# Layer 1's short form moved into layer 0's branch, with PE's order pinned and fillers in its waits

## The chip, the cores and the metric

The kernel runs on one core of a Trainium2 chip. The metric is the device time of one execution in microseconds (us). The engines are TensorE (PE in the profile; its weight loads are PEld), VectorE (DVE), ScalarE (ACT), GpSimd (POOL) and SyncE (SP), which issues most of the DMAs.

## The reference, cut to what matters

Four layers work on 2048 tokens of 256 features; each adds to the tokens what a conditioning step and a feed-forward step make of them.

```
x = x + L0_ffn(L0_cond(x, cond))     # 32 experts, top 1, and a shared expert
x = x + L1_ffn(L1_cond(x, cond, mask))
x = x + L2_ffn(L2_cond(x, cond))     # shared and routed experts, twice
x = x + L3_ffn(L3_cond(x, cond))     # shared and routed experts, then 16 experts
```

Layer 1 matters here. Its conditioning is an attention whose query is the same for all tokens of a batch of 1024:

```
a    = einsum('bhe,bhse->bhs', tp, q)          # tp: the condition
qmod = broadcast(einsum('bhs,bhse->bhe', a, q))  # one query for all
attn = softmax(where(mask, qmod.k / sqrt(e), neg))
o    = einsum('bhts,bhse->bhte', attn, v) @ Wo.T
```

Where all rows of the mask are equal, every token of a batch gets the same row `o`. Layer 1's feed-forward (a gate over 16 experts with q, k, v and o projections, and a causal attention with weights that sum to one) then also gives one row for each of the two batches. Layer 1 so comes down to two rows, each added to 1024 tokens. The kernel computes at run time whether the rows of the mask differ.

## The kernel before, in words

The tokens lie in SBUF twice: XT by channel (two halves of 128 channels, 2048 tokens) and Xt by token (16 tiles of 128 tokens by 256). A "ring" of 20 pieces of SBUF takes the weights of all layers in turn. The kernel is written in a tile framework: it tracks the data between instructions and puts in the semaphore waits. Each engine runs its own instructions in order. A scheduler sets that order, within one block between branches, from priorities that follow the order of the program; `_behind` pins one instruction after another with an order-only dependency. A branch ends the block on all engines: each jumps by itself, and the scheduler moves nothing across it.

Layer 0 (`_layer0`, from L385) computes the experts' logits and gives every expert 96 rows; `_route_static` also returns `nov`, how many of 21 overflow slots the tokens beyond 96 per expert need. Blocks 0 and 1 of the shared expert run (`shared(tb)`, 512 tokens each), then `_layer1_pre` (L593), which prepares what layer 1 needs of its weights and computes `differ`, the count of places in which the mask's rows differ. Then come 24 static slots (L470 to L483; `Split` does the matmuls, L1475 to L1493). Behind them `n` is loaded into a register on every engine (L484) and nested branches follow (`more`, L486 to L494): three overflow slots in each, as far as `n` goes. With these inputs `n` is 0: the slots' tokens are gathered into `xs` 138 times in all, 24 for layer 0's slots and 114 for the later layers'. Every engine jumps over the overflow code once.

Then layer 1's expert weights are loaded (`_layer1_experts`, L579: 16 loads of 512 KB, on SP), and blocks 2 and 3 of the shared expert run, with `Combine` (L1268) in their hooks: it gathers the slots' products from `ybuf` by row, adds them to Xt on DVE and transposes Xt back to XT (`_back`, L1258: ps_bk on PE, a copy on ACT). The loop of `_shared` (L1227) is, for every 128 hidden features: spg and spu (two matmuls each, L1240), Silu on ACT to ssg (L1245), the product sa on DVE (L1247), four spo matmuls (L1250).

Then `differ` is loaded and the second branch follows (L2095 to L2109): a general layer 1, or else the short form `_layer1_one` (L674). With these inputs the short form runs. It is a chain of small steps, each a few matmuls, then DVE or ACT on the product, then the next. In order, with the tiles' names: s_pa and s_v_t, s_v_o (attention weights over tokens, `by_block` and `over_tokens`), s_v_h, s_pq, s_pw (the query), s_psc, s_pm (scores, maximum), s_z_t, s_pr1, s_z_o (softmax, weighted tokens), s_z_h, s_po, s_ph (the row `o`), s_pn, s_pl (gate: norm, logits; a chain of some thirty small DVE steps follows, L821 to L858, and ends in s_hs), s_pk (L863, 32 matmuls with the experts' projections), s_pa2, s_pqk, s_pr (L890), s_pc, s_pb. Float32 matmuls have two records each in the profile. s_pc gives the two rows by channel, s_pb by token. L903 to L909 add them: eight ACT activations with a bias on XT, two DVE additions on Xt with s_pb read from PSUM. The weights for layer 2's shared expert are loaded in the same branch (`_shared_loads`; the profile has them under `_wload`'s line, L84).

Behind the branch layer 2 begins: `_shared` on XT (spg waits for the XT activations), and on DVE some twenty small memsets and preparations of later steps (L195 to L1756).

`_consts` also makes two bf16 constants, `iota16` and `one16`, that only layer 3's last step (`Last`, L1699) reads. `_warm` (L1216) issues bf16 matmuls of an identity with itself, 512 columns, of which nothing is read; before, layer 3 alone uses it (16 of them).

Of the kernel before, what the change touches and what calls it, by code (L numbers as in the profile page):

```python
# [86 lines left out]
def _consts(k):  # L87
# [24 lines left out]
    k.iota16 = cp.tile([P, CAP], BF16, name="iota16")  # L112
    nc.vector.tensor_copy(k.iota16, ii)
# [8 lines left out]
    k.one16 = cp.tile([P, P], BF16, name="one16")  # L122
    nc.vector.memset(k.one16, 1.0)
# [261 lines left out]
def _layer0(k):  # L385
# [5 lines left out]
    xbuf, ybuf = k.xbuf, k.ybuf  # L391
    with ExitStack() as ctx:
# [49 lines left out]
        rows, eid, nov = _route_static(k, rp, psum, ixf, E, C, NOV, "l0")  # L442
# [9 lines left out]
        def shared(tb, hook=None):  # L452
            po = _shared(k, pool, psum, HT, tb, *shw, hook)
            for i in range(2):
                t = tb * 4 + i * 2
                nc.vector.tensor_tensor(Xt[:, t:t + 2, :], po[i], Xt[:, t:t + 2, :], ALU.add)

        def weights(src):
            ws = [k.ring.take().rearrange("p (c f) -> p c f", f=f) for f in (F, F, D)]
            for w, n in zip(ws, ("L0_r1", "L0_r3", "L0_r2")):  # L460
                nc.sync.dma_start(w, A[n][src].rearrange("o (c p) f -> p (o c) f", p=P))
            return ws

        for tb in range(2):
            shared(tb)
        _layer1_pre(k, k.pre, psum)
        _router_biases(k, psum)
# [15 lines left out]
        split.finish()  # L483
        n = nc.values_load(nov[0:1, 0:1], min_val=0, max_val=NOV)  # L484
# [10 lines left out]
        k.l1w = _layer1_experts(k)  # L495
        k.yrows = (NS + NOV) * T
# [3 lines left out]
        k.ring.drop(hold)  # L500
        c.finish()


def _route_static(k, pool, psum, ixf, E, C, nov, name):
# [46 lines left out]
    rows = pool.tile([P, NT], U32, name=name + "_rows", tag="s_rows")  # L551
# [7 lines left out]
    eid = pool.tile([1, nov], I32, name=name + "_eid", tag="s_eid")  # L559
    nc.vector.tensor_copy(eid, ef)  # L560
    n = pool.tile([1, 1], I32, name=name + "_nov", tag="s_nov")
    nc.vector.tensor_copy(n, end[0:1, E - 1:E])
    return rows, eid, n
# [15 lines left out]
def _layer1_experts(k):  # L579

    r = k.ring.take(12).rearrange("p (n i e c f) -> n i p e c f", n=3, i=4, c=2, f=P)
    for i in range(4):
        for j, n in enumerate("qkv"):
            k.nc.sync.dma_start(r[j, i], k.A["L1_p" + n][i * 4:(i + 1) * 4]
                                .rearrange("e (c p) f -> p e c f", p=P))
    o = []
    for i in range(4):
        o.append(k.ring.take().rearrange("p (e f) -> p e f", f=D))
        k.nc.sync.dma_start(o[i], k.A["L1_po"][i * 4:(i + 1) * 4].rearrange("e p f -> p e f"))
    return r.rearrange("n i p e c f -> p n i e c f"), o  # L590


def _layer1_pre(k, pp, psum):  # L593
# [6 lines left out]
    with ExitStack() as ctx:  # L600
# [19 lines left out]
        nc.tensor.matmul(pd, k.ones, d1, start=True, stop=True)  # L620
        k.differ = pp.tile([P, 1], I32, name="l1_differ")
        nc.vector.tensor_copy(k.differ, pd)
# [51 lines left out]
def _layer1_one(k):  # L674
# [5 lines left out]
    l1w, l1o = k.l1w  # L680
    with ExitStack() as ctx:
        pool = ctx.enter_context(tc_pool(k, "l1s", 1))
        psum = ctx.enter_context(tc_pool(k, "l1sps", 2, PSUM))
# [27 lines left out]
        def by_block(w, name):  # L711

            ps = psum.tile([P, TB], F32, name=name, tag="b")
            for c in range(2):
                for g in range(4):
                    nc.tensor.matmul(ps[quad[g], :], w[:, c, g // 2, :], XT[:, c, g * TB:(g + 1) * TB],
                                     start=c == 0, stop=c == 1, skip_group_check=True)
            return ps

        def over_tokens(a, name):  # L720

            pt = psum.tile([P, 4, P], F32, name=name + "_t", tag="b")
            for j in range(4):
                nc.tensor.transpose(pt[:, j, :], a[:, j * P:(j + 1) * P], k.ident)
# [3 lines left out]
            ps = psum.tile([P, D], F32, name=name + "_o", tag="b")  # L728
            for j in range(4):
                for g in range(4):  # L730
                    nc.tensor.matmul(ps[quad[g], :], at[:, j, quad[g]], Xt[:, 4 * g + j, :],
                                     start=j == 0, stop=j == 3, skip_group_check=True)
            return ps

        def halves(x, name):

            ps = psum.tile([P, 2, 2, 16], F32, name=name + "_h", tag="s")
            for c in range(2):
                nc.tensor.matmul(ps[:, c].rearrange("p b h -> p (b h)"), x[:, c * P:(c + 1) * P],
                                 s2.rearrange("p b h -> p (b h)"), start=True, stop=True)  # L740
# [4 lines left out]

        pa = by_block(k.u, "s_pa")
        at = pool.tile([P, TB], F32, name="s_a")
        nc.scalar.copy(at[:, 0:256], pa[:, 0:256])
        nc.vector.tensor_copy(at[:, 256:TB], pa[:, 256:TB])
        pv = over_tokens(at, "s_v")  # L750
        vp = pool.tile([P, D], F32, name="s_vp")
        nc.vector.tensor_copy(vp, pv)
        v = halves(vp, "s_v")
        pq = psum.tile([P, 2, 2, 8], F32, name="s_pq", tag="s")
        for d in range(2):
            for c in range(2):
                nc.tensor.matmul(pq[:, d], w["q"][:, c, d * P:(d + 1) * P],
                                 v[:, c, :, 8 * d:8 * d + 8], start=c == 0, stop=c == 1)
# [3 lines left out]
        pw = psum.tile([P, 2, 2, 2, 8], F32, name="s_pw", tag="s")  # L762
        for c in range(2):
            for d in range(2):
                nc.tensor.matmul(pw[:, c, d].rearrange("p b j -> p (b j)"),
                                 k.natk[:, d, c * P:(c + 1) * P],
                                 qmd[:, d].rearrange("p b j -> p (b j)"), start=True, stop=True)
# [3 lines left out]
        psc = by_block(wk, "s_psc")  # L771
        sm = pool.tile([P, TB], F32, name="s_sm")
        mx = pool.tile([P, 1], F32, name="s_mx")
        nc.vector.tensor_tensor_reduce(sm, mb, psc, 1.0, -BIG, ALU.add, ALU.max, mx)
        pm = psum.tile([P, 1], F32, name="s_pm", tag="s")
        nc.tensor.matmul(pm, sw, mx, start=True, stop=True)
# [4 lines left out]
        pz = over_tokens(sm, "s_z")  # L781
        pr1 = psum.tile([P, 1], F32, name="s_pr1", tag="s")
        nc.tensor.matmul(pr1, sw, rs, start=True, stop=True)
# [6 lines left out]
        pov = psum.tile([P, 2, 2, 8], F32, name="s_po", tag="s")  # L790
        for d in range(2):
            for c in range(2):
                nc.tensor.matmul(pov[:, d], w["v"][:, c, d * P:(d + 1) * P],
                                 zT[:, c, :, 8 * d:8 * d + 8], start=c == 0, stop=c == 1)
# [5 lines left out]
        ph = psum.tile([P, 2, 2], F32, name="s_ph", tag="s")  # L800
        for i in range(2):
            for d in range(2):
                nc.tensor.matmul(ph[:, i, :], w["o"][:, d, i * P:(i + 1) * P], o[:, d, :],
                                 start=d == 0, stop=d == 1)
# [8 lines left out]
        pn = psum.tile([P, 2], F32, name="s_pn", tag="s")  # L813
        for c in range(2):
            nc.tensor.matmul(pn, k.ones, hq[:, c, :], start=c == 0, stop=c == 1)
        pl = psum.tile([P, 2, E], F32, name="s_pl", tag="s")
        for b in range(2):
            for c in range(2):
                nc.tensor.matmul(pl[:, b, :], hb[:, c, b, :], k.sim[:, c, :], start=c == 0, stop=c == 1)
# [39 lines left out]
        pk = psum.tile([P, 3, P], F32, name="s_pk", tag="b")  # L859
        for i in range(4):  # L860
            for c in range(2):
                for g in range(4):
                    nc.tensor.matmul(pk[quad[g]], hs[:, c, 4 * i + g, :], l1w[:, :, i, g, c, :],  # L863
                                     start=i == 0 and c == 0, stop=i == 3 and c == 1,
                                     skip_group_check=True)
# [3 lines left out]
        pa2 = psum.tile([P, 2], F32, name="s_pa2", tag="s")  # L869
        nc.tensor.matmul(pa2, pks[:, 2, :], r32[:, 0:2], start=True, stop=True)  # L870
# [3 lines left out]
        pqk = psum.tile([P, 2, P], F32, name="s_pqk", tag="s")  # L874
        nc.tensor.matmul(pqk, a4.rearrange("p g r -> p (g r)"), pks[:, 0:2], start=True, stop=True)
# [11 lines left out]
        pr = psum.tile([P, D], F32, name="s_pr", tag="b")  # L887
        for i in range(4):
            for g in range(4):
                nc.tensor.matmul(pr[quad[g], :], as_[:, 4 * i + g, :], l1o[i][:, g, :],  # L890
                                 start=i == 0, stop=i == 3, skip_group_check=True)
# [3 lines left out]
        pc = psum.tile([P, 2, 2], F32, name="s_pc", tag="s")  # L895
        for c in range(2):
            nc.tensor.matmul(pc[:, c, :], row[:, c * P:(c + 1) * P], r32[:, 0:2], start=True, stop=True)
        col = pool.tile([P, 2, 2], F32, name="s_col")
        nc.vector.tensor_copy(col, pc)
        pb = psum.tile([P, 2, D], F32, name="s_pb", tag="s")  # L900
        for b in range(2):
            nc.tensor.matmul(pb[:, b, :], ab[:, b, :], row, start=True, stop=True)
        for g in range(4):  # L903
            for c in range(2):
                x = XT[:, c, g * TB:(g + 1) * TB]
                nc.scalar.activation(x, x, AF.Identity, bias=col[:, c, g // 2:g // 2 + 1])  # L906
        for b in range(2):
            x = Xt[:, b * 8:(b + 1) * 8, :]
            nc.vector.tensor_tensor(x, x, _bc(pb[:, b, :], 1, [P, 8, D]), ALU.add)  # L909
# [306 lines left out]
def _warm(k, psum, ref, n):  # L1216

    ps = psum.tile([P, TB], F32, name="warm", tag="mm")
# [39 lines left out]
def _back(k, psum, src, dst, t, ref=None):  # L1258
# [6 lines left out]
    k.nc.scalar.copy(dst[:, :, t * P:(t + 1) * P], ps)  # L1265


class Combine:  # L1268
# [30 lines left out]
    def finish(self):  # L1299
# [894 lines left out]
```

## Time and profile before

| what | us |
|---|---|
| median of 3 runs (lowest, highest) | 1596.07 (1593.62, 1598.03) |
| the profiled execution | 1608.57 |
| its span, first to last instruction | 1606.7 |
| last layer 0 slot's matmuls (fpo, L1493) | 273.72 to 275.65 |
| first spg of shared(2) | 278.45 |
| last ps_bk of Combine | ends 329.71 |
| short form on PE, s_pa to s_pb | 334.77 to 385.94 |
| first spg of layer 2, first spo | 390.67, 397.29 |
| layer 1's loads issued by SP | 278.32 to 300.7 |

The mean granted TensorE clock of the profiled execution is 0.965 of full speed. The profiled execution is one execution, 12.5 us above the median of the runs without a profile. A group's line gives the busy time of all its instructions, the mean of one in ns, and behind the second bar the idle time of the engine ahead of them with what ended it. "issue" means that the profile shows no wait that ended it. PEldq, DVEq and so on are the sequencers of the engines, whose branch instructions are not counted as busy.

### The profile page before, as it was taken

What the parts mean: (1) busy time and instruction counts of PE and PEld (TensorE: products, weight loads), DVE (VectorE), ACT (ScalarE), POOL (GpSimd) and SP (SyncE); (2) the same over time, 40 slices, a digit from 0 to 9 for tenths busy, and PEclk for the clock granted to TensorE, in tenths of its full rate; (3) what the DMA queues carried; (4) which work ended last, traced back from release to release, by engine and by line L of the source; (5) the groups of instructions that cost most, each with busy time, mean ns of one, the idle gap of its engine ahead of it and who ended that gap; (6) DMA issues with size and microseconds to landing.
All of it is one profiled execution on the core that took longest, in us unless ns stands there. A gap on an engine that the chain in (4) does not pass through costs nothing. (4 is left out here: it accounts for less than half of the span.)

```text
span 1606.7 us, 23696 instructions
## 1 busy us (share of the span) xinstructions
PE 1484.9 (92%) x8602; PEld 1028.1 (64%) x8602; DVE 474.1 (30%) x1591; ACT 303.8 (19%) x641; POOL 285.0 (18%) x317
## 2 busy tenths in 40 slices
PE   5989998977999989999999999999999989998897
PEld 2543333533555876555599999999985548865575
DVE  3732221223411344341111111111114414446432
ACT  2312211112111212111111111111112212125222
POOL 0400000300231332023100000000000253410341
PEclk9889999977999999999999999999999999998899
DMA  9769994713211465051152354154507437662470
GB/s 251 255 206 338 345 315 157 254 54 119 81 52 40 142 214 180 27 190 53 34 179 87 119 183 150 51 181 177 177 14 266 140 121 246 193 203 92 138 242 22
DMA packets 184243, 252.47 MB, mean 157 GB/s; under 512 B 17112, under 2 KB 137824, under 8 KB 184113
## 3 DMA queue, kind: packets, MB, share of 16 engines
q1 hardware_dynamic: 164448, 210.92, 40.1%
q0 software_dynamic: 14176, 36.63, 6.3%
q10 hardware_dynamic: 5488, 3.25, 0.6%
q8 instruction: 74, 1.21, 0.3%
q14 instruction: 57, 0.46, 0.1%
HBM read 284.86 MB, written 50.76 MB: 209 GB/s over the span
## 5 line engine op out<-in xcount | busy, mean ns | idle before, releaser
L1250 PE MATMUL spo<-ring,sa 128*128 128x256 f32 x768 | 193.7, 395 | 20.2 <-DVE sa L1247 16.5
L285 POOL DMA_INDIRECT tbuf<-ys,sdst x114 | 112.3, 985 | 537.9 <-ACT ys L1453 228.4
L1250 PEld LDWEIGHTS spo<-ring,sa 128*128 128x128 f32 x768 | 141.2, 192 | 102.4 <-DVE sa L1247 75.2
L1247 DVE TENSOR_TENSOR sa<-ssg,spu 128x512 f32<-128x512 f32 x96 | 65.9, 686 | 340.8 <-PE spu L1240 289.3
L1444 PE MATMUL fpg<-xsT,ring 128*128 128x128 f32 x1152 | 141.6, 276 | 5.9 <-ACT ys L1453 5.9
L1444 PEld LDWEIGHTS fpg<-xsT,ring 128*128 128x128 f32 x1152 | 135.8, 192 | 10.4 <-ACT ys L1453 9.4
L1444 PE MATMUL fpu<-xsT,ring 128*128 128x128 f32 x1152 | 140.4, 275 | 0.0
L1444 PEld LDWEIGHTS fpu<-xsT,ring 128*128 128x128 f32 x1152 | 134.4, 192 | 0.0
L1448 DVE TENSOR_TENSOR fa<-fsg,fpu 128x512 f32<-128x512 f32 x72 | 49.5, 688 | 276.9 <-PE fpu L1444 276.9
L1451 PE MATMUL fpo<-ring,fa 128*128 128x256 f32 x576 | 130.3, 379 | 0.0
L1245 ACT ACTIVATE ssg<-spg 128x512 f32<-128x512 f32 x96 | 57.3, 597 | 348.4 <-PE spg L1240 242.8
L1451 PEld LDWEIGHTS fpo<-ring,fa 128*128 128x128 f32 x576 | 106.7, 190 | 13.0
L1240 PE MATMUL spg<-HT,ring 128*128 128x512 f32 x192 | 100.0, 608 | 5.1 <-PEq L488 2.8
L1240 PE MATMUL spg<-XT,ring 128*128 128x512 f32 x192 | 99.7, 609 | 4.7 <-ACT XT L906 4.7
L1427 PE MATMUL cpo<-ring,ch 128*128 128x256 f32 x312 | 86.7, 401 | 5.7 <-ACT ch L1424 4.1
L1240 PE MATMUL spu<-HT,ring 128*128 128x512 f32 x192 | 90.6, 592 | 0.0
L1240 PE MATMUL spu<-XT,ring 128*128 128x512 f32 x192 | 90.4, 593 | 0.0
L1421 PEld LDWEIGHTS cph<-xsT,ring 128*128 128x128 f32 x624 | 81.7, 191 | 5.0 <-ACT ch L1424 1.1
L1421 PE MATMUL cph<-xsT,ring 128*128 128x128 f32 x624 | 82.4, 275 | 0.7 <-ACT ch L1424 0.7
L1394 DVE COPY xsT<-ps_cm 128x256 f32<-128x256 f32 x138 | 56.7, 421 | 86.0 <-PE ps_cm L362 79.8
L1447 ACT ACTIVATE fsg<-fpg 128x512 f32<-128x512 f32 x72 | 43.0, 597 | 179.6 <-PE fpg L1444 179.6
L1427 PEld LDWEIGHTS cpo<-ring,ch 128*128 128x128 f32 x312 | 53.1, 189 | 20.4 <-ACT ch L1424 13.5
(570 smaller groups left out, 1601.0 us busy)
## 6 DMA issues: line engine op xcount, KB each, us to landing
ring<-in_L_w SPq DMA_DIRECT2D x108, 1024.0 KB
ring<-in_L_r SPq DMA_DIRECT2D x96, 512.0 KB
ring<-in_L_r SPq DMA_DIRECT2D x156, 256.0 KB
xs<-xbuf SPq DMA_DIRECT2D x138, 129.0 KB
ring<-in_L_W SPq DMA_DIRECT2D x32, 512.0 KB
yt<-tbuf SPq DMA_DIRECT2D x48, 256.0 KB
xbuf<-ACC SPq DMA_DIRECT2D x1, 6063.0 KB
ring<-in_L_s SPq DMA_DIRECT2D x6, 512.0 KB
```

The lines of the kernel that those rows point to most:

```text
L285: i = k.nc.gpsimd.indirect_dma_start(out=self.ap, out_offset=bass.IndirectOffsetOnAxis(ap=idx, axis=0), in_=rows, in_offset=None, **end)
L1240: mm = nc.tensor.matmul(ps, W[:, c, f * P:(f + 1) * P], X[:, c, cols], start=c == 0, stop=c == 1)
L1245: nc.scalar.activation(sg, pg, AF.Silu)
L1247: mul = nc.vector.tensor_mul(a, sg, pu)
L1250: mm = nc.tensor.matmul(po[g // 2][:, g % 2, :], a[:, g * P:(g + 1) * P], W2[:, f, :], start=f == 0 and g % 2 == 0, stop=f == nf - 1, skip ...
L1394: turned = nc.vector.tensor_copy(xT, _channel_major(k, self.psum, xs))
L1421: nc.tensor.matmul(ph[:, f, :], R1[:, c, f * P:(f + 1) * P], xT[:, c, :], start=c == 0, stop=c == 1)
L1427: nc.tensor.matmul(po, h[:, f, :], R2[:, f, :], start=f == 0, stop=f == 1)
L1444: nc.tensor.matmul(ps[:, j, :], W[:, c, (f0 + j) * P:(f0 + j + 1) * P], xT[:, c, :], start=c == 0, stop=c == 1)
L1447: nc.scalar.activation(sg, pg, AF.Silu)
L1448: nc.vector.tensor_mul(a[:, f0:f0 + 4, :], sg, pu)
L1451: nc.tensor.matmul(po, a[:, f, :], W2[:, f, :], start=f == 0, stop=f == 4 * nh - 1)
```

## The change

1. The first branch asks one combined question, `rare`: overflow slots or a mask with unequal rows. It is computed from `differ` and the total of the overflow (`end`) by two small DVE operations ahead of the slots. The Then side holds all that is seldom needed: the overflow slots, blocks 2 and 3, and a second branch for layer 1's form. The Else side holds the loads of layer 1's weights, blocks 2 and 3 with `Combine`, layer 2's loads and the short form, in one block. The order of pieces in the ring is kept; the loads alone stand inside.
2. In the short form every matmul is pinned behind the one before it (`pe`), from the last transpose of `Combine` on, and `fill(n)` puts n matmuls of `_warm` into the order: 4, 2, 1, 2, 1, 1, 1, 3, 4, 1, 2, 1, 2, 1, 14, 2, 2 and 6, 50 in all. On PE they follow: nothing (4), s_pa (2), s_v_t (1), s_v_o (2), s_v_h, s_pq, s_pw (1 each), s_psc (3), s_pm (4), s_z_t with s_pr1 (1), s_z_o (2), s_z_h (1), s_po (2), s_ph (1), s_pl (14), s_pk (2), s_pr (2), s_pb (6).
3. The two rows are copied to SBUF, into HT, which is free by then: the one by channel by DVE from s_pc, the one by token by ACT from s_pb. The additions (`_layer1_add`) stand behind the branch, common to both sides: eight ACT activations, two DVE additions from SBUF. On the general side the rows are zero.
4. `iota16` and `one16` are made in `Last`, which puts them on DVE right behind the branch, ahead of the additions on Xt.

Behind the branch the instructions are otherwise the same on every engine.

```diff
@@ _layer0
+        rare = k.pre.tile([1, 1], F32, name="l0_raref")
+        nc.vector.tensor_tensor(rare, k.differf[0:1, :], end[0:1, E - 1:E], ALU.add)
+        any_ = k.pre.tile([1, 1], I32, name="l0_rare")
+        nc.vector.tensor_copy(any_, rare)
...
+    def rest():
+        _layer1_loads(k)
         c = Combine(k, pool, psum, rows, Xt, XT, [0, 0] + [4] * 8, 2, 4)
         for tb in range(2, NB):
             shared(tb, c.hook(tb))
-        k.ring.drop(hold)
-        c.finish()
+        return c.finish()
+
+    def one(ref):
+        _shared_loads(k, k.l2, "L2_s1", "L2_s3")
+        _layer1_one(k, psum, ref)
+        _shared_loads(k, k.l2[2:], "L2_s2")
+
+    rare = nc.values_load(any_[0:1, 0:1], min_val=0, max_val=1 << 21)
+    with k.tc.If(rare > 0) as cmp:
+        with tc_pool(k, "l0p", 2) as pool, tc_pool(k, "l0ps", 4, PSUM) as psum:
+            slots_over()
+            rest()
+        differ = nc.values_load(k.differ[0:1, 0:1], min_val=0, max_val=1 << 20)
+        with k.tc.If(differ > 0) as cmp1:
+            _layer1_general(k)
+            _shared_loads(k, k.l2, "L2_s1", "L2_s3", "L2_s2")
+        with cmp1.Else():
+            with tc_pool(k, "l1sps", 4, PSUM) as psum:
+                one(None)
+    with cmp.Else():
+        with tc_pool(k, "l0p", 2) as pool, tc_pool(k, "l0ps", 4, PSUM) as psum:
+            one(rest())
+    _layer1_add(k)
@@ new
+def _layer1_sums(k):
+    return (k.HT[:, 1, 0:4].rearrange("p (c b) -> p c b", b=2),
+            k.HT[:, 0, 0:2 * D].rearrange("p (b d) -> p b d", d=D))
+
+def _layer1_add(k):
+    nc, (col, row) = k.nc, _layer1_sums(k)
+    for g in range(4):
+        for c in range(2):
+            x = k.XT[:, c, g * TB:(g + 1) * TB]
+            nc.scalar.activation(x, x, AF.Identity, bias=col[:, c, g // 2:g // 2 + 1])
+    for b in range(2):
+        x = k.Xt[:, b * 8:(b + 1) * 8, :]
+        nc.vector.tensor_tensor(x, x, _bc(row[:, b, :], 1, [P, 8, D]), ALU.add)
@@ _layer1_one
+    def pe(i):
+        nonlocal last
+        if last is not None:
+            _behind(k, i, last)
+        last = i
+
+    def fill(n):
+        nonlocal last
+        if last is not None:
+            last = _warm(k, psum, last, n, tag="o", bufs=2)
...
+        fill(4)
         pa = by_block(k.u, "s_pa")
+        fill(2)
...
         pm = psum.tile([P, 1], F32, name="s_pm", tag="t", bufs=2)
-        nc.tensor.matmul(pm, sw, mx, start=True, stop=True)
+        pe(nc.tensor.matmul(pm, sw, mx, start=True, stop=True))
+        fill(4)
...
+        fill(14)
         hn = pool.tile([P, 2], F32, name="s_hn")
...
         for b in range(2):
-            nc.tensor.matmul(pb[:, b, :], ab[:, b, :], row, start=True, stop=True)
-        for g in range(4):
-            for c in range(2):
-                x = XT[:, c, g * TB:(g + 1) * TB]
-                nc.scalar.activation(x, x, AF.Identity, bias=col[:, c, g // 2:g // 2 + 1])
-        for b in range(2):
-            x = Xt[:, b * 8:(b + 1) * 8, :]
-            nc.vector.tensor_tensor(x, x, _bc(pb[:, b, :], 1, [P, 8, D]), ALU.add)
+            pe(nc.tensor.matmul(pb[:, b, :], ab[:, b, :], row, start=True, stop=True))
+        fill(6)
+        nc.scalar.copy(rows, pb)
@@ _consts, Last.__init__
-    k.iota16 = cp.tile([P, CAP], BF16, name="iota16")
-    nc.vector.tensor_copy(k.iota16, ii)
-    k.one16 = cp.tile([P, P], BF16, name="one16")
-    nc.vector.memset(k.one16, 1.0)
+        k.iota16 = rp.tile([P, CAP], BF16, name="iota16")
+        k.nc.vector.tensor_copy(k.iota16, k.iota)
+        k.one16 = rp.tile([P, P], BF16, name="one16")
+        k.nc.vector.memset(k.one16, 1.0)
```

## The prediction

> **What bounds the kernel now.** I read the page first, for the engine that bounds; then the windows of the branches and of layer 1's short form; then its groups of instructions; last the timeline of its end.
>
> ```profile
> PE 1484.9 (92%) x8602; PEld 1028.1 (64%) x8602; DVE 474.1 (30%) x1591; ACT 303.8 (19%) x641; POOL 285.0 (18%) x317
> PEclk9889999977999999999999999999999999998899
> ```
>
> TensorE is busy for 92% of the span. The second line is the granted clock by fortieths (40.2 us each): it dips in the 9th and 10th, 321 to 402 us, where the short form lies.
>
> The windows (columns: stretch, length, busy time by engine with counts, granted clock, DMA share, GB/s):
>
> ```profile
> 278.45:300.00 21.55, 21.55 (x57) 11.13 (x58) 3.46 (x7) 2.39 (x4) 6.88 (x8) 0.92 1.03 316
> 329.72:334.77 5.05, 0.00 (x1) 0.00 (x1) 0.11 (x2) 0.40 (x2) 0.00 (x0) 0.84 0.53 208
> 334.77:338.40 3.63, 3.63 (x16) 0.59 (x16) 2.77 (x10) 0.00 (x0) 0.00 (x0) 0.50 0.04 9
> 344.00:346.60 2.60, 1.70 (x12) 1.49 (x12) 0.72 (x3) 0.00 (x0) 0.00 (x0) 1.00 0.00 0
> 346.60:356.80 10.20, 7.43 (x32) 4.11 (x32) 1.59 (x9) 1.18 (x3) 0.00 (x0) 0.51 0.00 0
> 363.80:372.45 8.65, 4.56 (x20) 4.39 (x20) 4.83 (x35) 1.72 (x3) 0.00 (x0) 0.50 0.01 2
> ```
>
> Three things are to be seen: 5.05 us before the short form in which nothing computes; a clock of about 0.50 over most of it; and a busy PE that gains nothing from being busy, since each product waits for a vector step and the next vector step for the product.
>
> The groups (busy us, mean ns | idle before):
>
> ```profile
> L863 PE MATMUL s_pk<-ring,s_hs 128*32 128x384 f32 x64 | 7.9, 662 | 3.6 <-DVE s_hs L858 3.6
> L716 PE MATMUL s_psc<-XT,s_wk 128*32 128x512 f32 x16 | 3.6, 1061 | 0.3 <-DVE s_wk L769 0.3
> L731 PE MATMUL s_z_o<-Xt,s_z_at 128*32 128x256 f32 x32 | 3.6, 634 | 0.3 <-ACT s_z_at L726 0.3
> L716 PE MATMUL s_pa<-XT,l_u 128*32 128x512 f32 x16 | 3.6, 1058 | 5.1 <-issue 5.1
> ```
>
> The branch instructions of PE's sequencer, first for layer 0's overflow (L488), then for layer 1 (L2097), durations in ns:
>
> ```profile
> L488 PEldq COMPARE_BRANCH  x1: 3348/3348/3348, 274.8 to 274.8; - x1
> ```
> ```profile
> L2097 PEldq COMPARE_BRANCH  x1: 4972/4972/4972, 329.7 to 329.7; - x1
> ```
>
> The end, from the timeline:
>
> ```profile
> 385.20 5.01 ACT L906 ACTIVATE XT<-XT,s_col 128x512 f32<-128x512 f32 x8 [2.25 <-DVE s_col L899]
> 385.97 4.49 DVE L909 TENSOR_TENSOR Xt<-Xt,s_pb 128x2048 f32<-128x2048 f32 x2 [0.81 <-PE s_pb L902]
> 390.67 3.75 PE L1240 MATMUL spg<-XT,ring 128*128 128x512 f32 x4 [4.74 <-ACT XT L906]
> 394.58 1.28 ACT L1245 ACT_TABLE_LOAD   x1 [4.37 <-PE spg L1240]
> 396.50 0.69 DVE L1247 TENSOR_TENSOR sa<-ssg,spu 128x512 f32<-128x512 f32 x1 [4.77 <-ACT ssg L1245]
> 397.29 0.89 PE L1250 MATMUL spo<-ring,sa 128*128 128x256 f32 x3
> ```
>
> PE idles 4.74 us for eight additions on ACT, then runs at half clock, and ACT loads its table only after the first spg.
>
> [...]rises at 343.2, 360.3 and 377.3 lie whole multiples of 3.41 us apart, and 344.0 to 346.6 (1.70 us of small products) was followed by 0.51.[...]
>
> **The change, part by part.** Times are on the axis of the profiled execution (span 1606.7, 1.9 us around it: 1608.57). It lies 12.5 us above the median of 1596.07; I take the difference over to the median, since no term scales with the span.
>
> *1. One branch where the first was.* [...]I price the jump at the 4.97 us row: PE goes on at 274.8 + 5.0 = 279.8 in place of 278.45, **+1.35**. Bounds: at 3.35 us, less L488's own steps, −0.3. Above, layer 1's loads: SP takes the same branch early and can issue about five 512 KB loads by 276[...]: 7 us, +3.5. DVE passed the old branch at once and now jumps too; it has some 3.1 us of layer 1's preparation (2.77 by 338.4) moved ahead: about 283. ACT's branch at 277.0 plus 6 is 283. The first spu is ready near 285, so both are hidden under PE's first products; each us beyond 285 shows in full. POOL and SP go through long before. The L2 loads stay behind the same waits on spg and spo. The two small DVE operations for the combined flag (about 0.1 us each, s_col's COPY is 0.16) lie ahead of the slots, under PE.
>
> *2. The second branch goes.* From the end of ps_bk (329.71) to s_pa were 5.06 us. Now four fillers (4 × 0.213 = 0.85; a 512-column bf16 product of L1220 takes 0.425 us each in the run of ten at half clock, 4.43 us in all, and half that at full) run while ACT copies the last XT (0.42): 0.9. **−4.15.**
>
> *3. Fifty fillers hold the clock.* Full-clock prices: 1.92 us for sixteen 32-row products of 512 columns (ps_lt, L1195), the same for 32 of 256 columns (fpo, L1493), four transposes 0.66, pk 0.082 for a record after 377.3, 0.60 for four small products, 1.05 for eight. Gains: s_pa and s_psc 1.72 each, z_o 1.71, v_o 1.32, pk 2.63, pw 0.81, ph 0.76, pn and pl 0.71, z_t 0.45, v_t 0.25, pm 0.21: 12.3 if the clock holds throughout. The fillers fit the waits at full speed: one or two (0.21, 0.43) into waits of 0.27 to 0.66, three (0.64) into 0.82, four into 1.29, fourteen (2.98) into 3.6. But between z_h and pl, about 5.6 us, there are only small products and 0.85 us of filler. The small products of 344 to 346.6 did not hold the clock, so I expect a drop there. It gives back 0.76 and 0.71, and runs the fourteen partly at half speed: entirely at half they take 5.95, 2.35 over their wait; the clock should rise on the way, so about 0.75. Together 2.2 back: **−10.1**. The like stretch v_h to pw has more filler; I let it hold (2.0 if not). Bounds −12.3 and −6.
>
> *4. The row is added behind the branch.* s_pb, at 385.94 on the old axis, is copied by ACT (0.6, as ssg) before the eight activations: 386.7 to 391.7. Then the table load 1.28 and ssg 0.6: 393.6. DVE's additions wait for that copy, 386.8 to 391.3; with 1.3 us of memsets and 0.2 us for the two moved constants it is free before 393.6. So sa at 393.6 and spo at 394.55 in place of 397.29: **−2.75**. PE needs only two of the activations and does the six spg and spu products at full clock by about 391; what is late next is ACT. The jump to the common code lies under this. Bounds −3.3 (copy and join cheap) and −1 (PE cools in its new idle time of 3 us, 1.7 us).
>
> Sum: 1.35 − 4.15 − 10.1 − 2.75 = **−15.65**: 1580.4.
>
> **Rivals.** *Full clock everywhere*: −12.3 in place of −10.1, 1578.2; with a cheap branch 1576.5. For it: at 104.1 to 107.5 PE was busy for 3.01 of 3.4 us, with small products, and kept its clock. *The clock held in the large products only[...]*: −6 for step 3, +3.5 for step 1 and −1 for step 4 are −7.65, 1588.4. *The other side: the fillers never lift the clock and become work.* At 0.425 us they exceed the waits they sit in by 5.3 us (fourteen by 2.35, four by 0.41, three by 0.45, the rest 0.1 to 0.4 each), the first four cost 0.85 more, and the products that before ran at full clock (pk's second half 2.6, pr 1.7, pqk and pa2 0.5) lose 4.8: +11, with the others' −5.55 a time of 1601.5. It decides from a clock term above +5.55. Against it: with no filler at all the dense pk raised the clock at 377.3. *The change doesn't do its work* because the fillers run outside the waits: step 3 zero, −5.55, 1590.5.
>
> **How the numbers follow.** Forecast (1577 to 1585) 0.55; full clock 0.15; weak hold[...] (1585 to 1591) 0.20; around no change, a part of the last two rivals, 0.06; the other side 0.04. A measurement can tell about 0.3% (4.8 us) from no change: faster 0.90, same 0.06, slower 0.04. The range for 8 in 10 runs from 1576 (full clock, cheap branch) to 1589[...].
>
> **What would show it.** One long COMPARE_BRANCH on PE near 275, of 3.3 to 7 us, and none near 330; s_pa within 1 us of ps_bk; s_pa, s_psc and z_o at 1.9 us rather than 3.6; a clock of 0.9 or more to z_h and a dip between z_h and pk; pk in 5.2 us; spo released by sa, with ACT's table load directly behind the last XT activation. Wrong would be: 3.6 us for these products, the fourteen fillers ending over 1 us after s_hs, sa late in shared(2), or PE idle for over 4 us before spo.

## The result, and the profile after

The changed kernel took 1587.72 us (median of 12 runs, 1582.27 to 1591.17), the kernel before beside it 1594.44 (12 runs, 1591.68 to 1599.47): a ratio of 0.9951, 95% interval 0.9934 to 0.9967, or 7.8 us less (5.3 to 10.5; the two medians lie 6.7 apart). 1580.4 had been forecast, 15.65 us less.

The page of the changed kernel and its windows (stretch, length, busy time by engine, granted clock, DMA share, GB/s):

```profile
PE 1487.3 (94%) x8652; PEld 1027.9 (65%) x8652; DVE 474.6 (30%) x1594; ACT 304.2 (19%) x642; POOL 284.4 (18%) x317
...
PEclk9889999999999999999999999999999999999899
```
```profile
273.46:278.72 5.26, 0.01 (x2) 0.03 (x1) 0.49 (x4) 0.37 (x1) 0.00 (x0) 0.85 1.17 323
329.73:330.53 0.80, 0.80 (x6) 0.20 (x3) 0.00 (x0) 0.41 (x2) 0.00 (x0) 1.00 0.73 241
...
334.30:338.70 4.40, 4.24 (x47) 2.50 (x48) 1.07 (x3) 1.28 (x1) 0.00 (x0) 1.00 0.01 4
338.70:346.00 7.30, 6.63 (x44) 2.94 (x43) 1.71 (x9) 1.13 (x3) 0.00 (x0) 1.00 0.00 0
...
350.60:360.30 9.70, 9.48 (x39) 5.41 (x38) 5.35 (x38) 1.72 (x3) 0.00 (x0) 0.65 0.01 2
...
377.30:383.00 5.70, 3.42 (x8) 2.82 (x9) 1.16 (x13) 1.45 (x2) 0.00 (x0) 0.70 0.04 15
```

The dip in the clock's line is gone. PE's gap at the branch is 5.26 us where it was 2.80, with the DMA queues full (1.17). The gap ahead of the short form is 0.80 us and filled. The clock is 1.00 through the short form but for 350.6 to 360.3, where the small products stand; it is 0.70 in the stretch around the first spo behind it.

The same products as before, in the changed kernel's groups, and its branch on PE's sequencer:

```profile
L961 PE MATMUL s_pk<-ring,s_hs 128*32 128x384 f32 x64 | 5.4, 488 | 0.0
...
L817 PE MATMUL s_z_o<-Xt,s_z_at 128*32 128x256 f32 x32 | 1.9, 382 | 0.2 <-ACT s_z_at L812 0.2
...
L799 PE MATMUL s_pa<-XT,l_u 128*32 128x512 f32 x16 | 1.9, 598 | 0.0
L799 PE MATMUL s_psc<-XT,s_wk 128*32 128x512 f32 x16 | 1.9, 598 | 0.1
```
```profile
L522 PEldq COMPARE_BRANCH  x1: 5802/5802/5802, 272.8 to 272.8; - x1
```

The end, from the timeline:

```profile
371.85 5.01 ACT L738 ACTIVATE XT<-XT,HT 128x512 f32<-128x512 f32 x8
...
372.43 4.47 DVE L741 TENSOR_TENSOR Xt<-Xt,HT 128x2048 f32<-128x2048 f32 x2
...
372.73 1.95 PE L1335 MATMUL spg<-XT,ring 128*128 128x512 f32 x4
...
376.87 1.28 ACT L1340 ACT_TABLE_LOAD   x1
...
378.80 0.69 DVE L1342 TENSOR_TENSOR sa<-ssg,spu 128x512 f32<-128x512 f32 x1 [1.02 <-ACT ssg L1340]
...
379.58 3.62 PE L1345 MATMUL spo<-ring,sa 128*128 128x256 f32 x8 [2.33 <-issue]
```

spg starts after two of ACT's eight additions, at full clock. Then sa waits for ssg, ssg for the table load, that for the eighth activation on ACT. PE idles for 2.33 us and its clock drops (0.50 from 379.52 to 382.93): the first spo takes 3.62 us, where the kernel before has 1.97.

From the end of the slots to the first spo the trace has 121.64 us before and 106.12 after: 15.5 less, against a sum of 15.65; the 1.65 us that the first spo then takes longer lie behind this stretch. The step that did not carry was from there to the kernel's time. The experiments ask where the gain comes from and why the whole kernel shows only half of it.

### The profile page after: what moved, and what is told of

It reads as the page before. It is cut to its first block, busy times and chain, and to the rows that moved or that the text cites. A ratio compares the mean times of both kernels' runs of the same rounds, so it can differ in the third digit from the quotient of the medians.

```text
span 1586.0 us, 23805 instructions
## 1 busy us (share of the span) xinstructions
PE 1487.3 (94%) x8652; PEld 1027.9 (65%) x8652; DVE 474.6 (30%) x1594; ACT 304.2 (19%) x642; POOL 284.4 (18%) x317
## 5 line engine op out<-in xcount | busy, mean ns | idle before, releaser
L1542 PEld LDWEIGHTS fpg<-xsT,ring 128*128 128x128 f32 x1152 | 135.8, 192 | 10.4 <-ACT ys L1551 9.4
```

Source lines behind the costliest of these rows:

```text
L1542: nc.tensor.matmul(ps[:, j, :], W[:, c, (f0 + j) * P:(f0 + j + 1) * P], xT[:, c, :], start=c == 0, stop=c == 1)
```

## The experiments

Theory A: the profiled execution of before had bad luck with the clock, and a usual one loses less in the short form. Rivals: the gain is made and given back behind layer 1 (B); the fillers gain little. The chips differ: the kernel before took 1592.52 us on the chip of the first four runs, 1608.17 on that of the next four, 1603.9 on that of the last, so each run is compared with the kernel before on its own chip. The expectations of the first four give times on the scale of the first pair (1594.4 and 1587.7).

**The kernel before again**, unchanged.

> The kernel before, unchanged, profiled anew. Theory A (the profiled execution of before was an unlucky one: [...]its short form ran at half clock nearly throughout, and a usual execution loses less there): about 1594.5, the stretch from s_pa to s_pb 44 to 48 us in place of 51.2, and a mean clock above 0.965. Theory B (the short form always takes 51 us in before, and what the change gains there is given back behind it): 1594.5 too, but s_pa to s_pb 50.5 to 52 us at the same clock of about 0.5, and the 12 us that this profile is above the median lie in other stages.

1593.72 us (14 runs); the profiled execution 1599.38, at 1597.5 of span. s_pa to s_pb took 51.10 us, and in two more traces of this code 51.19 and 51.18. So in every trace of before the short form is as slow as in the first. But none of these four is of a quick execution: the first lies above all twelve runs beside it, this one is the slowest of its 14, the other two the middle and the slowest of theirs. For these theory A falls; for quick executions it is untested.

**No fillers.**

```diff
     def fill(n):
-        nonlocal last
-        if last is not None:
-            last = _warm(k, psum, last, n, tag="o", bufs=2)
+        return
```

> The changed kernel without its 50 fillers, all else kept. The predicted worth of the fillers is 10.1 us: 1597.8 from 1587.7, slower than the kernel before. Theory A (half of that is luck that a usual execution has without fillers): 4 to 7 us, 1591.7 to 1594.7. Theory B (the fillers gain 10 in layer 1 and lose part behind it): 1591 to 1594 as well, but with s_pa to s_pb 50 us or more in the profile, and the stages behind spo shorter than with fillers.

1582.12 us, ratio 0.9939 (0.9916 to 0.9962): not told apart from the changed kernel's 0.9951, and below what either theory gave. Its groups on PE:

```profile
L960 PE MATMUL s_pk<-ring,s_hs 128*32 128x384 f32 x64 | 6.7, 583 | 3.6 <-DVE s_hs L955 3.6
L798 PE MATMUL s_psc<-XT,s_wk 128*32 128x512 f32 x16 | 3.6, 1061 | 0.3 <-DVE s_wk L860 0.3
L798 PE MATMUL s_pa<-XT,l_u 128*32 128x512 f32 x16 | 2.4, 598 | 0.0
L816 PE MATMUL s_v_o<-Xt,s_v_at 128*32 128x256 f32 x32 | 1.9, 382 | 0.5 <-ACT s_v_at L811 0.5
```

Without any filler, and with no jump ahead of them, s_pa and s_v_o run at full clock: 1.00 from 326.61 to 332.80, and 598 and 382 ns a product where the kernel before has 1058 and 634. s_psc is back at 1061 ns. s_pa to s_pb took 45.5 us where the kernel before has 51.1. The three windows, in the kernel before, without fillers and in the changed kernel (the last column but two is the granted clock):

```profile
334.77:385.94 51.17, 39.44 (x268) 20.48 (x268) 14.85 (x76) 7.53 (x14) 0.00 (x0) 0.65 0.14 51
```
```profile
326.61:372.14 45.53, 33.91 (x269) 18.37 (x268) 12.26 (x67) 7.27 (x14) 0.00 (x0) 0.78 0.20 77
```
```profile
330.53:371.33 40.80, 39.06 (x310) 19.44 (x310) 12.28 (x67) 6.79 (x12) 0.00 (x0) 0.92 0.22 80
```

In the traces of before and after the granted clock is 1.00 or 0.50 (before: 0.50 from 333.15, 1.00 from 343.39, 0.50 from 346.80, 1.00 from 360.45), so a mean of 0.65 over 51.17 us means 36 us at half clock; read in the same way it is 20 without fillers, in the changed kernel 7. More than half of what step 3 put on the fillers comes without them, with the removal of the branch. 3.0 us are gained up to s_v_h, in the products that ran at half clock behind the jump; the rest comes later in the chain, where the half-clock stretches fall otherwise. The pinning of PE's order is no rival here: the order of the short form's products is the same in both traces.

**Fillers in the kernel before**, 46 of them, with the order pinned; one place stands for all.

```diff
-        pm = psum.tile([P, 1], F32, name="s_pm", tag="s")
-        nc.tensor.matmul(pm, sw, mx, start=True, stop=True)
+        pm = psum.tile([P, 1], F32, name="s_pm", tag="t", bufs=2)
+        pe(nc.tensor.matmul(pm, sw, mx, start=True, stop=True))
+        fill(4)
...
```

> The kernel before with the pinned order and 46 fillers in its short form (the four ahead of s_pa left out, since the branch stands there), branch and additions as before. By the prediction's step 3, less what the cold start after the branch keeps (s_pa 1.7, s_v_t and s_v_o up to 1.6): 10.1 - 3.3 = 6.8 us off the kernel before, 1587.6. Theory A: 3 to 5 us off, 1589.5 to 1591.5. If fillers were worth nothing: 1594.4.

1590.34 us, ratio 0.9995 (0.9982 to 1.0009): no gain that can be told from nothing (at most 2.9 us), where 6.8 had been worked out. Yet its trace has 42.35 us from s_pa to s_pb and a first spo 112.5 us after the slots (122.8 in the trace of before on this chip). The two traces come from opposite ends: this profiled execution, 1586.33, is the quickest of its 14, that of before, 1599.38, the slowest of its 14.

**The additions back inside the branch**, from PSUM.

```diff
         fill(6)
-        nc.scalar.copy(rows, pb)
+        for g in range(4):
+            for c in range(2):
+                x = XT[:, c, g * TB:(g + 1) * TB]
+                nc.scalar.activation(x, x, AF.Identity, bias=col[:, c, g // 2:g // 2 + 1])
+        for b in range(2):
+            x = Xt[:, b * 8:(b + 1) * 8, :]
+            nc.vector.tensor_tensor(x, x, _bc(pb[:, b, :], 1, [P, 8, D]), ALU.add)
...
-    _layer1_add(k)
```

> The changed kernel with the additions of the two rows back inside the branch, straight from PSUM, as in the kernel before. The prediction's step 4 puts 2.75 us on having them behind the branch: 1590.5. Rival (PE cools in its new wait ahead of spo, seen as a first spo at half clock, and gives most of it back): 1588 to 1589. If the jump to the common code behind the additions is not covered any more: up to 5 us more, 1592.5.

1585.13 us, ratio 0.9962 (0.9947 to 0.9978), not told apart from the changed kernel's 0.9951, so its time decides nothing on step 4. In its trace the first spo comes 11.04 us after s_pb and takes 1.97; in the changed kernel 8.25 and 3.62. Of the 2.8 us, 1.65 are lost again to the slower spo, which stands at a clock of 0.50.

**The kernels cut off** behind two shared blocks of layer 2, so that the stretch is measured in many runs and not in one trace. In each:

```diff
-        _layer2_cond(k)
-        _layer2_ffn(k)
-        _layer3(k)
+        last = Last(k)
+        last.head()
+        for tb in range(2):
+            po = _shared(k, k.pool, k.psum, k.XT, tb, *k.l2, 8)
+            for i in range(2):
+                t = tb * 4 + i * 2
+                nc.vector.tensor_tensor(k.Xt[:, t:t + 2, :], po[i], k.Xt[:, t:t + 2, :], ALU.add)
+        nc.sync.dma_start(k.out.rearrange("(t p) d -> p t d", p=P), k.Xt)
```

(`head` is `begin` up to its memsets, without its DMAs.)

> The kernel before cut off behind two shared blocks of layer 2 (layer 2's routed part and its feed-forward and all of layer 3 left out, so that the output is not the reference's), in order that the stretch around the change stands alone with many runs. Base for the three beside it. Theory A (clock luck of the profiled executions): its runs spread over 8 us or more, with the clock, and the fastest ones are those with the higher clock. Theory C (the spread of the whole kernel comes from the stages behind): spread below 4 us.

490.32 us (6 runs, five of them from 488.8 to 491.5, one at 483.07). Theory C falls. The spread of 8.4 us and the quickest run at the highest mean clock (0.925) are what theory A had named, though another run took 490.4 at 0.924.

> The changed kernel cut off in the same place. If the traces' stretch from the last slot to the first spo (before 121.6 and 122.8 us, after 106.1) holds on the average: 15 to 17 us below the cut kernel before. If the gain of the whole kernel (7 us) is all that is made here too: 6 to 9 us below.

476.95 us (476.52 to 477.77): 13.4 less by the medians, 12.0 by the means, neither the 15 to 17 of the trace nor the 6 to 9 of the whole kernel. Its branch took longer than any other traced:

```profile
L522 PEldq COMPARE_BRANCH  x1: 7786/7786/7786, 270.4 to 270.4; - x1
```

> The changed kernel without fillers, cut off in the same place. By the traces (110.6 us in this stretch against 106.1): 4 to 5 us slower than with fillers. By the whole kernel's times (1582.1 without, 1587.7 with): no slower than with them, perhaps 2 to 5 us faster. If the second holds here, the fillers bring nothing in the stretch itself; if the first holds, they gain here and lose behind it.

479.23 us (476.69 to 481.68): the fillers' own part in the changed kernel is 2.3 us by the medians, less than the 4 to 5 of the traces and within the spread of these five runs.

> The kernel before with 46 fillers, cut off in the same place. By the traces (112.5 us against 122): 9 to 10 us below the cut kernel before. By the whole kernel's times: 0 to 2 us below.

483.16 us (482.77 to 484.61): 7.2 less by the medians, 5.8 by the means, between the two expectations and close to the 6.8 worked out for fillers behind a jump. All five runs lie where the quickest run of the cut kernel before lies.

**Whole and cut kernels on one chip.** The changed kernel and the two cut ones, unchanged.

> The changed kernel once more, beside the cut kernels on one chip, since the chips differ by up to 16 us in the kernel before. Theory A (the gain is as large in the whole kernel as in the cut one[...]): its gain on the kernel before equals that of the cut pair beside it within 2.5 us. Theory B (part is given back in the stages behind): 7 us here where the cut pair shows 12 to 14.

1593.99 us against 1603.9, ratio 0.9941 (0.9922 to 0.996): 9.5 us less (6.4 to 12.5).

> The cut kernel before (layer 2's routed part and feed-forward and layer 3 left out), on the chip of the whole kernels beside it. On the other chip: 490.3 us, five of six runs within 488.8 to 491.5. Theory A: 484 to 491, near 490 only where the whole kernel before is near 1608. Theory B: 490 wherever.

488.82 us (484.56 to 490.03). Two of the five took 484.56 and 485.07 us, at a mean clock of 0.925 and 0.929; the other three 488.8 to 490.0, at 0.916.

> The changed kernel cut in the same place, same chip. Both theories: 476 to 478, since the fillers take the chance out of the clock.

475.35 us (470.81 to 478.36): 13.5 less by the medians, 12.5 by the means, close to the other chip. The spread of 7.6 us on this chip is against the expectation that fillers take the chance out of the clock. The whole kernel shows 4 us less gain beside it (3 by the means), more than theory A allowed and less than theory B asked.

**The additions drawn apart**, since ACT adds to tokens that nobody needs yet while the first spo waits.

```diff
-    for g in range(4):
...
+    def later(act, mul):
+        b = 2 - len(k.later)
+        cols((range(1, 2), range(2, 4))[b], act)
         x = k.Xt[:, b * 8:(b + 1) * 8, :]
-        nc.vector.tensor_tensor(x, x, _bc(row[:, b, :], 1, [P, 8, D]), ALU.add)
+        i = nc.vector.tensor_tensor(x, x, _bc(row[:, b, :], 1, [P, 8, D]), ALU.add)
+        _behind(k, i, mul)
+
+    cols(range(1))
+    k.later = [later, later]
...
```

(`cols` issues the activations of the blocks of 512 tokens that it is given, pinned behind `act`: two for the first block at once, six later. `_shared` calls `later` behind its first and second sa.)

> The changed kernel with the additions behind the branch drawn apart: only the two activations that the first 512 tokens need stand ahead of layer 2's first Silu, two follow behind that Silu and four behind the second; one addition on Xt stands behind the first sa, one behind the second. If the first spo waits for ACT and DVE to add to tokens that nobody needs yet, it comes 2 to 3 us earlier and at full clock, and the kernel gains 3 to 4 us on the changed one. If the wait is given back at the later activations (the logits of layer 2 need all of XT): 0 to 1 us.

1590.01 us (6 runs), ratio 0.9904 to the kernel before (0.9877 to 0.9931), 4 us below the changed kernel beside it, as the first of the two expectations had it; the intervals of the two ratios still overlap. Its timeline, with s_pb ending at 368.81:

```profile
369.33 1.33 ACT L740 ACTIVATE XT<-XT,HT 128x512 f32<-128x512 f32 x2
...
372.24 1.28 ACT L1351 ACT_TABLE_LOAD   x1 [1.57 <-issue]
373.53 0.60 ACT L1351 ACTIVATE ssg<-spg 128x512 f32<-128x512 f32 x1
...
374.16 0.69 DVE L1353 TENSOR_TENSOR sa<-ssg,spu 128x512 f32<-128x512 f32 x1 [3.09 <-ACT ssg L1351]
374.77 2.29 DVE L748 TENSOR_TENSOR Xt<-Xt,HT 128x2048 f32<-128x2048 f32 x1
...
374.95 1.97 PE L1359 MATMUL spo<-ring,sa 128*128 128x256 f32 x8 [0.21 <-issue]
```

spo comes 6.14 us after s_pb instead of 8.26: the six later activations on ACT were the wait. DVE's additions were not, for in the changed kernel DVE had been idle for 1.02 us when sa began. The clock gains nothing here: the first spo takes 1.97 us in both traces of this chip. The version's ratio to the kernel before is the lowest of all.

## Why the prediction was right or wrong

The stretch, from the traces (us; "to spo's end" runs from the end of ps_bk to the end of the first eight spo records):

| trace | slots to spg | ps_bk to s_pa | s_pa to s_pb | s_pb to spo | spo | to spo's end |
|---|---|---|---|---|---|---|
| before, first | 2.80 | 5.06 | 51.17 | 11.35 | 1.97 | 69.6 |
| before, again | 4.18 | 5.13 | 51.10 | 11.36 | 1.97 | 69.6 |
| before, cut | 2.86, 3.22 | 5.19, 5.19 | 51.19, 51.18 | 11.34, 11.30 | 1.99, 1.99 | 69.7, 69.7 |
| after | 5.26 | 0.80 | 40.80 | 8.25 | 3.62 | 53.5 |
| after, again | 5.56 | 0.80 | 40.79 | 8.26 | 1.97 | 51.8 |
| after, cut | 7.24, 5.38 | 0.79, 0.79 | 40.97, 42.46 | 8.21, 8.21 | 3.61, 3.68 | 53.6, 55.1 |
| no fillers | 5.42 | -0.07 | 45.53 | 8.96 | 1.97 | 56.4 |
| no fillers, cut | 5.40 | -0.07 | 44.34 | 8.21 | 1.99 | 54.5 |
| before, fillers | 2.89 | 5.14 | 42.35 | 11.22 | 1.97 | 60.7 |
| before, fillers, cut | 2.90 | 5.52 | 44.77 | 11.03 | 1.99 | 63.3 |
| after, additions inside | 5.43 | 0.79 | 40.80 | 11.04 | 1.97 | 54.6 |
| after, late additions | 5.40 | 0.79 | 42.32 | 6.14 | 1.97 | 51.2 |

- **Step 1, the branch (+1.35).** Mis-sized: 3.3 us on the average of the four traces of before became 5.9 in the four after, +2.6. The value and its bound of 3.5 were my estimates. As the bound assumed, the jump runs beside layer 1's loads (DMA share 1.17), and COMPARE_BRANCH took 5.8 to 7.8 us; that the loads lengthen it is not shown. I should have taken the value nearer that bound.
- **Step 2 (−4.15).** Measured −4.3. But it was priced as idle time alone. PE also came out of the jump at half clock (0.50 in the first trace of before): without the jump and without fillers the short form takes 44.3 to 45.5 us instead of 51.2.
- **Step 3 (−10.1).** The size was right (51.17 to 40.80, −10.4) and so was its pattern: the clock dropped between z_h and pk (0.65), s_hs was ready at 359.30 and pk began at 360.34, 1.0 late where 0.75 was worked out (0.6 to 1.3 in the four traces; over 1 had been named as a sign against it). The cause was wrong: the step gave all of it to the fillers. Of the 10.4 us, 5.6 to 6.9 come with step 2; the fillers add 2 to 5 in the short form, and the cut kernels show 2.3. The size came out because what the missing jump earned was booked here. Behind a jump, in the kernel before, the fillers bring 6.4 and 8.8 us in the traces.
- **Step 4 (−2.75).** Measured −3.1, and +1.65 in three of four traces in the first spo itself (3.61 to 3.68 us instead of 1.97), which stood in the bounds and not in the value. In the changed kernel's trace PE was busy for 1.15 of the 3.41 us from 376.11 to 379.52, at a clock of 1.00, and the next 3.41 us stand at 0.50. In the fourth trace PE idles as long, 2.34 us, and its spo takes 1.97; what decides between the two is not shown.

From ps_bk to spo's end the four traces of before average 69.6 us and the four after 53.5: −16.1, and with the branch −13.5. The sum of 15.65 was 2 us too large, in the branch's term and in the tail's.

That the cut kernels measured −13.4 and −13.5 is in part chance. In their own traces, from the end of the slots to spo's end, the changed kernel is only 10.9 and 11.5 us shorter; its slots also end 3.0 and 3.7 us earlier, and no step of the prediction lies ahead of the branch. One part of this shows in all traces. In blocks 0 and 1 of layer 0's shared expert DVE waits for the last load of the mask, before and after:

```profile
88.13 2.29 DVE L615 TENSOR_TENSOR l_ne<-l_mm,l_m 128x2048 uint8<-128x2048 uint8 x1 [7.37 <-DMA l_mm<-in_mask]
```
```profile
87.91 2.29 DVE L653 TENSOR_TENSOR l_ne<-l_mm,l_m 128x2048 uint8<-128x2048 uint8 x1 [4.94 <-DMA l_mm<-in_mask]
```

In the six traces with the old layer 0 (with or without fillers) this wait is 6.9 to 7.5 us, in the eight with the new one 4.8 to 5.3, and PE, which waits for the sa behind it, idles 6.0 to 6.5 us against 4.4 to 4.9. So some 1.6 us come from a side effect of the edit ahead of the branch; which of the moved instructions makes it is not shown.

What failed is the sentence that took the difference over to the median: 15.5 us in one pair of traces, 7.8 in the runs. The measured time lies within the range of 1576 to 1589, but that is luck. It lies in the row from 1585 to 1591, which stood for a clock held only in the large products or a long jump; the jump was long, but by 1.3 us more than in the sum, and the changed kernel's trace shows the clock held nearly throughout the short form (0.92).

The profiled execution of before, 12.5 us above its median, was no exception in the stretch: three more traces agree within 0.2 us, though none is of a quick execution. Other stages vary too, in code that the change does not touch. Layer 3's conditioning, from l3c_pl to l3f_pt, took 171.2 us in the second trace of before, 181.2 in the first, 174.4 after and 184.9 in the second trace after. In the last, ACT and DVE start late, and the profile names no work of another engine that would account for it. From its timeline:

```profile
1268.98 0.60 ACT L1340 ACTIVATE ssg<-spg 128x512 f32<-128x512 f32 x1 [7.96 <-PE spu L1335]
...
1272.62 0.69 DVE L1342 TENSOR_TENSOR sa<-ssg,spu 128x512 f32<-128x512 f32 x1 [9.72 <-remote]
...
1273.36 2.93 PE L1345 MATMUL spo<-ring,sa 128*128 128x256 f32 x6 [4.98 <-DVE sa L1342]
```

The version with late additions, on the same chip, has the same 4.98 us in the same place; the four traces of the first chip have none. The first trace of before, of another pair, has the like: DVE idle for 8.27 and 6.58 us ahead of two sa, with the same "remote" behind it, the profile's word for a release that it can't place.

**What stays open** is the last 3 to 6 us. The cut kernels gain 13.4 and 13.5 by their medians, 12.0 and 12.5 by their means, the whole one 7.8 and 9.5. On one chip the difference is 3 to 4 us, and the scatter of the two medians (some 3 us for the cut pair, as much for the whole one) nearly covers it. Fillers in the kernel before gain 7.2 cut and nothing whole, on different chips; without fillers it is 11.1 cut and 9.7 whole.

That the gain is given back behind the first spo is not shown, and the traces of one chip speak against it: from the end of the first spo to the end of the span they have 1200.7 us before, 1198.5 with fillers in it, 1199.6 without fillers in the changed kernel, 1201.0 with the additions inside. The other reading is theory A for the quick executions. Three of eleven cut runs of before took 483 to 485 us, about as long as those with fillers, at the highest mean clocks of their set. In the whole kernel before the quick runs have the higher clock as well: of the 14 beside its second trace those below 1589 us had 0.974 and 0.975, the slowest 0.967. If the short form holds the clock in them without fillers, the medians of the runs must show less gain than these traces. No trace was taken of such an execution, so this is argued, not shown.

## What to carry to other kernels

In these traces the jump ahead of the chain cost more than its idle time of 5 us: PE came out of it at a clock of 0.50, and the chain of small products behind it won the full clock back only for short stretches (36 of 51 us at half clock). So try to put rare cases behind one branch and let the common path run on, before thinking of fillers. An edit also moves instructions ahead of the place that it is about: compare the stages in front as well. And a gain read from one trace is a gain in that stretch of that execution. Look where the traced execution lies among the runs, and measure what the whole kernel makes of it.

## What was not expected of the hardware

- The same kernel took 1592.5, 1603.9 and 1608.2 us on three chips. On the one with 1603.9, ACT and DVE started late in layer 3 in both traces, with no wait for data that the profile shows.
- A long COMPARE_BRANCH on PE beside full DMA queues: 5.8 to 7.8 us in eight traces at a DMA share of 1.05 to 1.15. In the kernels with the old branches it took 3.3 to 4.6 us at the first (share 0.14 to 0.15) and 5.0 to 5.5 at the second (0.47 to 0.54). The places differ too, so that the load on the queues is the cause is not shown.
- PE idle for 2.3 us, after 4.5 us of dense products at full clock, was followed by half the clock in three of four traces (the first spo took 3.61 to 3.68 us there, 1.97 in the fourth).
